# Pinning layer 2's loads, PSUM operands for the half sums and a mask by matmul in a four-layer graph network

## Chip, core and metric

The kernel runs on one core of a Trainium2 chip. The metric is the time of one execution on the device in microseconds (us), the median of several. The core has five engines that run their own instruction streams: TensorE (PE; its weight loads are shown apart as PEld), VectorE (DVE), ScalarE (ACT), GpSimd (POOL) and SyncE (SP), which here issues all DMA transfers.

## What is computed

Four graph layers follow each other over x, 32 batches of 512 nodes with 128 features. Each normalises, applies a relu and adds its result to x. All use one 512x512 matrix adj. Cut to what matters here:

```python
# layer 0: attention over the pattern of adj
m = adj > 0
idx = cumsum(m.reshape(-1)) - 1
A = where(m, e[0][idx], NEG)            # NEG = -9e15; e has 256 entries, an index past the end takes the last
A = softmax(A, axis=1)
out = (A * eye) @ h0 + (A * (1 - eye)) @ h1 + bias      # h0 = h W[0], h1 = h W[1]
# layer 1: x0, x0 adj and its Chebyshev step, each times a block of Theta, relu
# layer 2: weights = adj * adj; messages = weights^T relu(h psi); two dense layers
# layer 3: scores from h q k^T h^T, tanh, exp, times adj, divided by the row sum, times h v
```

## The kernel before

Two batches make a tile q (0 to 15). The 512x512 matrices are multiplied by a scheme of seven products per pair instead of eight, which needs sums and differences of the four 256x256 quarters of the left matrix ("half sums", `sum_steps`) and of the right one (`rt_...`). The preparation builds layer 0's attention matrix, its transpose `attT` and the half sums of that; then rounds `r` of layer 0 follow, two tiles each.

The loads that layers 2 and 3 need:

```python
def load_crossed(dst, src):
    for b in range(NQR):                       # NQR = 4
        nc.sync.dma_start(dst[:, b, :], src.rearrange("(a b c) w -> b a c w", a=NT, c=QR)[b])   # L99
# [cut]
def square():
    sq = square_tile("sq")                     # one of four 512x512 buffers
    load_crossed(sq, adj)
    adjTx.append(square_tile("adjTx"))
    load_crossed(adjTx[0], adjT_d)
    yield
    for i in range(NT):                        # sq becomes adj * adj, on GpSimd
        # [cut]
    yield from sum_steps(sq, "sq")
# [cut] the order in which the program is written from the last round of layer 0 on:
waiting = [[next_layer, layer0_last(), layer1(1)]]        # next_layer is layer1(0)
waiting += [[layer1(q)] for q in range(2, NQ)]
waiting[5].append(square())
# each iteration adds one entry and steps every active generator once
```

Engines PE, DVE, ACT and POOL run the preparation and all rounds of layer 0 but the last in the order of the source (a manual schedule). What follows is ordered by the scheduler of the framework, which works with modelled times; transfers are ordered by it throughout, except those that are pinned, as the later loads of x are.

In layer 0 the features of a tile reach their transposed form hT by VectorE's 32x32 transpose (`hb`), a transfer to DRAM (`d_hT`, L269) and one back (`hT`, L272); the first three tiles are transposed on TensorE. `p_g` (L385) is the product of hT and W[1].

Layer 0's mask and scores, in the preparation (`m` is 1 where adj > 0):

```python
att = square_tile("att")
for t in range(NT):                            # (m - 1) * -NEG: 0 where m is 1, 9e15 where it is 0 (least is sought)
    nc.gpsimd.tensor_scalar(att[:, t, :], m[:, t, :], -1.0, -NEG, OP.add, OP.mult)      # L455
# [cut]
nc.gpsimd.tensor_scalar(elastn, elast, -1.0, None, OP.mult)        # minus the last entry of e
us = [prep.tile([P, N], F32, tag="u", name=f"u_{t}", bufs=NT) for t in range(NT)]
def entries(t):
    nc.scalar.mul(us[t], m[:, t, :], elastn)                       # L521
    nc.gpsimd.tensor_add(att[:, t, :], us[t], att[:, t, :])        # L522
entries(0); entries(1)                         # [cut] entries(2), entries(3) after go(normal[0])
# [cut] normal[q]: the normalised h of tile q, eight ACT instructions (L230)
go(normal[1])
bias(0)                                        # a GpSimd addition to x (L395)
for kk in range(NK):                           # NK = 2
    nc.vector.tensor_scalar(at_row[:, kk, :], ...)                 # L565
    nc.vector.tensor_scalar(at_col[:, kk, :], ..., OP.is_equal, OP.mult)                # L566, 0 or -1
for kk in range(NK):
    for i in range(3):
        nc.vector.tensor_scalar(at_part[:, i, kk, :], ...)         # L569

def score_rows(t):
    ph = bank(f"p_first_{t}")                  # a PSUM bank
    for kk in range(NK):                       # L581: -1 at each of the first 256 entries
        nc.tensor.matmul(ph, at_row[:, kk, blk(t)], at_col[:, kk, :], start=(kk == 0), stop=(kk == NK - 1))
    pv = bank(f"p_val_{t}")                    # L585: six matmuls, the values of e in three bf16 parts
    # [cut]
def softmax_rows(t):
    ph, pv = scores[t]
    u = us[t]
    nc.vector.scalar_tensor_tensor(u, ph, elastn, att[:, t, :], OP.mult, OP.add)        # L592
    nc.vector.tensor_tensor_reduce(u, pv, u, ..., OP.add, OP.min, least[:, t : t + 1])  # L593
    nc.scalar.activation(u, u, AF.Exp, ...)                        # L594
```

The end of the preparation:

```python
pt = [bank(f"p_attT_{j}") for j in range(NT)]  # the transposed attention matrix, in four PSUM banks
# [cut] transposes, p_g of two tiles, rt_g of round 0 (GpSimd, L311), p_adiag
for j in range(NT):
    (nc.vector.tensor_copy if j % 2 else nc.scalar.copy)(attT[:, j, :], pt[j])          # L637
nc.scalar.copy(adiag, p)                       # L638
go(normal[2])                                  # eight ACT instructions
go(sum_steps(attT, "att", nc.vector))

def sum_steps(mat, name, eng=nc.gpsimd):
    a11, a12 = mat[:, 0:2, 0:H], mat[:, 2:4, 0:H]                  # H = 256
    a21, a22 = mat[:, 0:2, H:N], mat[:, 2:4, H:N]
    # [cut] s1, s2, s4: tiles in SBUF
    for out, op, p, q in ((s1, OP.add, a21, a22), (s2, OP.subtract, s1, a11),
                          (a21, OP.subtract, a11, a21), (s4, OP.subtract, a12, s2)):
        tc.keep_in_program_order(eng.tensor_tensor(out, p, q, op))                      # L290
        yield
```

Round 0 then takes products in the order a11 (`p_l_a`), s2 (`p_l_c`), s1 (`p_l_d`), the changed a21, a12, a22, s4 (L337). Ahead of the second TensorE transposes h[2] (`p_hT`, L248). `hd` (GpSimd, L656) feeds the diagonal's products (L709). `cheb` is layer 1's second matrix, also made along the way.

Of the kernel before, what the change touches and what calls it, by code (L numbers as in the profile page):

```python
# [9 lines left out]
F32 = mybir.dt.float32  # L10
F16 = mybir.dt.float16
BF16 = mybir.dt.bfloat16
AF = mybir.ActivationFunctionType
OP = mybir.AluOpType
AX = mybir.AxisListType

P = 128
QR = 32
# [6 lines left out]
def kernel(  # L25
# [37 lines left out]
    nc = tc.nc  # L63
    B, N, D = x.shape
    NT = N // P
    NE = e_l0.shape[1]
    NK = NE // P
    NQ = B // 2

    const = ctx.enter_context(tc.tile_pool(name="const", bufs=1))  # L70
# [6 lines left out]
    def bank(name):  # L77
        return psum.tile([P, 512], F32, tag="bank", name=name)
# [4 lines left out]
    def blk(t):  # L83
        return slice(t * P, (t + 1) * P)


    def square_tile(name):
        return const.tile([P, NT, N], F32, tag="square", name=name, bufs=4)
# [7 lines left out]

    def load_crossed(dst, src):
        for b in range(NQR):
            nc.sync.dma_start(dst[:, b, :], src.rearrange("(a b c) w -> b a c w", a=NT, c=QR)[b])  # L99

    adj_s = square_tile("adj_s")
    adj_r = adj.rearrange("(t p) j -> p t j", p=P)
# [37 lines left out]
    elast = const.tile([P, 1], F32, name="elast")  # L140
# [22 lines left out]
    prep = prep_scope.enter_context(tc.tile_pool(name="prep", bufs=1))  # L163
# [9 lines left out]
                   allow_small_or_imprecise_dtypes=True)  # L173
    ident = const.tile([P, P], F32, name="ident")
    make_identity(nc, ident)
    eps = const.tile([P, 1], F32, name="eps")
    nc.vector.memset(eps, EPS)
    nc.scalar.activation(prep.tile([P, 1], F32, name="powers"), eps, AF.Exp)
# [99 lines left out]
    H = N // 2  # L278
    sums = {}

    def sum_steps(mat, name, eng=nc.gpsimd):

        a11, a12 = mat[:, 0:2, 0:H], mat[:, 2:4, 0:H]
        a21, a22 = mat[:, 0:2, H:N], mat[:, 2:4, H:N]
        extra = const.tile([P, 3, 2, H], F32, tag="sums", name=f"sums_{name}", bufs=3)
        s1, s2, s4 = extra[:, 0], extra[:, 1], extra[:, 2]
        sums[name] = {1: a11, 2: a12, 3: s4, 4: a22, 5: s1, 6: s2, 7: a21}
        for out, op, p, q in ((s1, OP.add, a21, a22), (s2, OP.subtract, s1, a11),
                              (a21, OP.subtract, a11, a21), (s4, OP.subtract, a12, s2)):
            tc.keep_in_program_order(eng.tensor_tensor(out, p, q, op))  # L290
            yield

    def right_blocks(half, name, engs):

        right = {}
        for _ in right_steps(half, name, engs, right):
            pass
        return right
# [117 lines left out]
    def go(steps, n=99):  # L416
        for _ in range(n):
            if next(steps, steps) is steps:
                return
# [24 lines left out]
    m = prep.tile([P, NT, N], BF16, name="m")  # L444
# [4 lines left out]
    rch = prep.tile([P, NT], F16, name="rch")  # L449
    nc.vector.tensor_copy(rch, rc)  # L450


    att = square_tile("att")
    for t in range(NT):
        nc.gpsimd.tensor_scalar(att[:, t, :], m[:, t, :], -1.0, -NEG, OP.add, OP.mult)  # L455
    pt = [bank(f"p_adjT_{j}") for j in range(NT)]
# [8 lines left out]
    for t in range(NT):  # L465
        for s in range(t + 1):
            nc.tensor.matmul(pi[:, t : t + 1], upto[:, s, blk(t)], rch[:, s : s + 1],
                             start=(s == 0), stop=(s == t))
    pc = bank("p_count")
    for t in range(NT):  # L470
        nc.tensor.matmul(pc, rch[:, t : t + 1].to_broadcast([P, P]), upto[:, t, :],
                         start=(t == 0), stop=(t == NT - 1))
# [19 lines left out]
    for kk in range(NK):  # L492
        for t in range(NT):
            nc.tensor.matmul(pb[:, kk : kk + 1], of_row[:, t, blk(kk)], befh[:, t : t + 1],
                             start=(t == 0), stop=(t == NT - 1))
# [3 lines left out]
    at_row = prep.tile([P, NK, N], BF16, name="at_row")  # L499
    at_col = prep.tile([P, NK, N], BF16, name="at_col")  # L500
# [12 lines left out]
            nc.gpsimd.tensor_sub(ecoln, ecoln, part)  # L513
        parts.append(part)
    elastn = prep.tile([P, 1], F32, name="elastn")
    nc.gpsimd.tensor_scalar(elastn, elast, -1.0, None, OP.mult)

    us = [prep.tile([P, N], F32, tag="u", name=f"u_{t}", bufs=NT) for t in range(NT)]

    def entries(t):  # L520
        nc.scalar.mul(us[t], m[:, t, :], elastn)  # L521
        nc.gpsimd.tensor_add(att[:, t, :], us[t], att[:, t, :])  # L522

    entries(0)
    entries(1)
    for kk in range(NK):
        s = prep.tile([P, N], F16, tag="scr", name=f"scr_r{kk}", bufs=2)
        nc.vector.tensor_scalar(s, pc, rows[:, kk : kk + 1], None, OP.is_le, OP.add,
# [6 lines left out]
    for kk in range(NK):  # L535
        w = prep.tile([P, N], F32, tag="scan", name=f"scan_{kk}", bufs=1)
# [9 lines left out]
    project = [project_steps(q, hT[q], copies[q]) for q in range(3)]  # L546
    next(pieces[0], None)
    go(normal[0])
    entries(2)
    entries(3)  # L550
    next(pieces[1])
    next(pieces[1])
    next(pieces[1], None)
# [3 lines left out]
    p = bank("p_qk_t")  # L557
# [20 lines left out]
    def score_rows(t):  # L578
        ph = bank(f"p_first_{t}")
        for kk in range(NK):  # L580
            nc.tensor.matmul(ph, at_row[:, kk, blk(t)], at_col[:, kk, :], start=(kk == 0), stop=(kk == NK - 1))  # L581
        pv = bank(f"p_val_{t}")
        for kk in range(NK):
            for i in range(3):
                nc.tensor.matmul(pv, at_row[:, kk, blk(t)], at_part[:, i, kk, :], start=(kk == 0 and i == 0),  # L585
                                 stop=(kk == NK - 1 and i == 2))
        scores[t] = ph, pv

    def softmax_rows(t):
        ph, pv = scores[t]  # L590
        u = us[t]
        nc.vector.scalar_tensor_tensor(u, ph, elastn, att[:, t, :], OP.mult, OP.add)  # L592
        nc.vector.tensor_tensor_reduce(u, pv, u, 1.0, 3.0e38, OP.add, OP.min, least[:, t : t + 1])  # L593
        nc.scalar.activation(u, u, AF.Exp, bias=least[:, t : t + 1], scale=-1.0,  # L594
                             accum_out=total[:, t : t + 1])

    def scaled_rows(t, u):
        nc.vector.reciprocal(total[:, t : t + 1], total[:, t : t + 1])
        nc.scalar.mul(split(att[:, t, :]), crossed(u), total[:, t : t + 1])
        own = split(att[:, t, :])[:, :, t, :]  # L600
        d = diag[:, t, :].rearrange("p (b c) -> p b c", c=QR)
        nc.gpsimd.tensor_mul(d, own, ident.rearrange("p (b c) -> p b c", c=QR))
        nc.gpsimd.tensor_sub(own, own, d)

    for t in range(NT):
        score_rows(t)
# [3 lines left out]
    nc.tensor.matmul(p_qk[:, :D], qkT[:, 0, :], qkT[:, 1, :], start=True, stop=True)  # L610
    qk = const.tile([P, D], F32, name="qk")
    attT = square_tile("attT")
    for t in range(NT):
        softmax_rows(t)
        if t > 0:
            scaled_rows(t - 1, us[t - 1])
    next(turned[1], None)
# [3 lines left out]
    pt = [bank(f"p_attT_{j}") for j in range(NT)]  # L621
# [11 lines left out]
    p = bank("p_adiag")  # L633
    for t in range(NT):
        nc.tensor.matmul(p[:, blk(t)], ones, diag[:, t, :], start=True, stop=True)
    for j in range(NT):
        (nc.vector.tensor_copy if j % 2 else nc.scalar.copy)(attT[:, j, :], pt[j])  # L637
    nc.scalar.copy(adiag, p)  # L638
    go(normal[2])
    go(sum_steps(attT, "att", nc.vector))  # L640

    prep_scope.close()
    late = ctx.enter_context(tc.tile_pool(name="late", bufs=4))
# [21 lines left out]
    def late_sums():  # L665

        for name, mat in (("adj", adj_s), ("cheb", cheb)):
            yield from sum_steps(mat, name)
# [289 lines left out]
    def square():  # L958

        sq = square_tile("sq")  # L960
# [4 lines that stand above are left out]
        for i in range(NT):  # L965
            s = late.tile([P, N], F32, tag="hs", name=f"sq_{i}", bufs=4)
            nc.gpsimd.tensor_mul(split(s), crossed(sq[:, i, :]), crossed(sq[:, i, :]))
            nc.gpsimd.tensor_copy(sq[:, i, :], s)
        yield from sum_steps(sq, "sq")
# [54 lines left out]
```

## Time and profile before

| | |
|---|---|
| time, median of 3 (lowest, highest) | 986.16 us (985.79, 986.97) |
| span of the profiled execution | 984.6 us |
| mean granted TensorE clock | 0.997 |
| half sums of attT, VectorE, four instructions | 1.80, 1.64, 1.75, 1.75 us |
| m times elastn, ACT, four instructions in two pairs | 1.33 and 1.32 us a pair |
| u and att added, GpSimd, four instructions in two pairs | 2.50 and 2.54 us a pair |
| issues of sq, from | three at 161.83, one at 194.61 us |
| issues of adjTx, from | two at 204.78, two at 206.41 us |

The profile names a group by line, engine and operation, then what is written and read, its shape and how often. "Busy" is the time an engine executes; the time before it, in brackets or in a column, is idle time, with the instruction or transfer that ended it after an arrow. Starts are counted from the start of the span. A tenth row of 40 digits shows the busy share in 40 equal slices of the span.

### The profile page before, as it was taken

What the parts mean: (1) busy time and instruction counts of PE and PEld (TensorE: products, weight loads), DVE (VectorE), ACT (ScalarE), POOL (GpSimd) and SP (SyncE); (2) the same over time, 40 slices, a digit from 0 to 9 for tenths busy, and PEclk for the clock granted to TensorE, in tenths of its full rate; (3) what the DMA queues carried; (4) which work ended last, traced back from release to release, by engine and by line L of the source; (5) the groups of instructions that cost most, each with busy time, mean ns of one, the idle gap of its engine ahead of it and who ended that gap; (6) DMA issues with size and microseconds to landing.
All of it is one profiled execution on the core that took longest, in us unless ns stands there. A gap on an engine that the chain in (4) does not pass through costs nothing.

```text
span 984.6 us, 15193 instructions
## 1 busy us (share of the span) xinstructions
PE 965.6 (98%) x5473; PEld 788.0 (80%) x5474; DVE 597.3 (61%) x1363; ACT 469.6 (48%) x1059; POOL 402.7 (41%) x451
## 2 busy tenths in 40 slices
PE   7999997999999999999999999999999999999998
PEld 3789997889999999999977787777767776777776
DVE  8868887556556565566766666565555444444444
ACT  4675456103232232336766655554574554445553
POOL 6748798562226322221253344444133322233322
PEclk9999999899999999999999999999999999999999
DMA  9155554422213122135333343223132121121111
GB/s 257 49 144 156 150 150 134 128 82 65 66 43 86 43 65 65 47 86 147 86 110 103 115 123 108 74 77 87 44 93 77 46 75 55 54 76 43 54 33 43
DMA packets 83050, 87.10 MB, mean 88 GB/s; under 512 B 6816, under 2 KB 73120, under 8 KB 82976
## 3 DMA queue, kind: packets, MB, share of 16 engines
q1 hardware_dynamic: 82976, 86.14, 31.1%
q8 instruction: 43, 0.70, 0.3%
q14 instruction: 31, 0.25, 0.1%
HBM read 44.70 MB, written 41.42 MB: 87 GB/s over the span
## 4 chain that ended last, share of the span: by engine, by line
PE 93%; DVE 3%; DMA 2%; ACT 1%; issue 0%; SPq 0%; POOL 0%; DVEq 0%; ACTq 0%
PE p_av L944 12%; PE p_l L385 11%; PE p_score L929 11%; PE p_msgT_c L330 4%; PE p_x2T_c L330 4%; PE p_x1T_c L330 4%; PE p_l_c L337 4%; PE p_feat L385 3%; PE p_msgT_d L330 3%; PE p_x1T_a L330 3%; PE p_msgT_a L330 3%; PE p_hv L385 3%; PE p_x2T_d L330 3%; PE p_x1T_d L330 3%; PE p_x2T_a L330 3%; PE p_phi L899 3%
## 5 line engine op out<-in xcount | busy, mean ns | idle before, releaser
L230 ACT ACTIVATE h<-x,sh,rs 128x128 f32<-128x128 f32 x512 | 208.6, 483 | 91.5 <-PE p_x2T_d L330 46.9
L934 POOL TENSOR_TENSOR ex<-ex,adjTx 128x512 f32<-128x512 f32 x64 | 83.2, 1301 | 206.4 <-ACT ex L932 206.4
L930 ACT ACTIVATE ex<-p_score 128x512 f32<-128x512 f32 x128 | 71.8, 587 | 124.6 <-issue 113.0
L944 PEld LDWEIGHTS p_av<-qkh_hv,ex 128*128 128x128 f32 x1024 | 118.5, 191 | 9.4 <-issue 7.4
L944 PE MATMUL p_av<-qkh_hv,ex 128*128 128x129 f32 x1024 | 120.1, 275 | 0.8 <-POOL ex L934 0.8
L929 PE MATMUL p_score<-qkh_hv,hT 128*128 128x512 f32 x256 | 115.2, 593 | 0.0
L264 DVE STREAM_TRANSPOSE hb_hT<-h 128x512 f32<-128x512 f32 x122 | 83.1, 696 | 20.7 <-ACT h L230 20.4
L934 DVE TENSOR_TENSOR ex<-ex,adjTx 128x512 f32<-128x512 f32 x64 | 45.4, 709 | 81.7 <-ACT ex L932 81.7
L202 DVE BATCH_NORM_STATS2 bn<-x 128x6 f32<-128x256 f32 x256 | 93.0, 418 | 1.6
L929 PEld LDWEIGHTS p_score<-qkh_hv,hT 128*128 128x128 f32 x256 | 46.2, 190 | 46.5 <-issue 45.0
L385 PE MATMUL p_l<-th,x12T 128*128 128x128 f32 x512 | 78.1, 275 | 0.0
L932 ACT ACTIVATE ex<-ex 128x512 f32<-128x512 f32 x128 | 76.6, 630 | 1.8
L311 POOL TENSOR_TENSOR rt_h<-h 128x256 f32<-128x256 f32 x32 | 23.2, 726 | 114.1 <-PE p_x2T_d L330 66.6
L385 PEld LDWEIGHTS p_l<-th,x12T 128*128 128x128 f32 x512 | 67.5, 192 | 0.0
L311 POOL TENSOR_TENSOR rt_feat<-feat,feat 128x256 f32<-128x256 f32 x16 | 11.6, 724 | 126.2 <-ACT feat L882 126.2
L654 POOL COPY hs<-hT 128x512 f32<-128x512 f32 x32 | 19.5, 612 | 74.8 <-PE p_l L385 33.0
L385 PE MATMUL p_l<-th,hs 128*128 128x128 f32 x256 | 49.5, 275 | 0.0
L385 PEld LDWEIGHTS p_hv<-vw,hT 128*128 128x128 f32 x256 | 33.6, 192 | 15.3 <-issue 8.1
L894 POOL TENSOR_TENSOR x<-x,phi2b 128x256 f32<-128x256 f32 x64 | 44.9, 732 | 0.0
L358 ACT COPY x12T<-p_x1T_a 128x256 f32<-128x256 f32 x16 | 6.0, 372 | 74.4 <-PE p_x1T_a L330 74.4
L656 POOL TENSOR_TENSOR hd<-hT,adiag 128x512 f32<-128x512 f32 x32 | 41.0, 1312 | 0.0
L385 PEld LDWEIGHTS p_l<-th,hs 128*128 128x128 f32 x256 | 40.0, 192 | 0.8
(224 smaller groups left out, 1992.6 us busy)
## 6 DMA issues: line engine op xcount, KB each, us to landing
d_hT<-hb_hT SPq DMA_DIRECT2D x244, 128.0 KB, 2.4
hT<-d_hT SPq DMA_DIRECT2D x61, 512.0 KB, 3.4
x<-in_x_dram SPq DMA_DIRECT2D x32, 256.0 KB, 5.2
out_dram<-x SPq DMA_DIRECT2D x31, 256.0 KB, 2.3
adj_s<-in_adj_dram SPq DMA_DIRECT2D x4, 256.0 KB
adjT_d<-adjT SPq DMA_DIRECT2D x1, 1024.0 KB
sq<-in_adj_dram SPq DMA_DIRECT2D x4, 256.0 KB
adjTx<-adjT_d SPq DMA_DIRECT2D x4, 256.0 KB
```

The costliest lines, as they stand in the source:

```text
L202: nc.vector.bn_stats(st[:, k].rearrange("p e s -> p (e s)"), xt[q][:, b, t : t + 2, :].rearrange("p t f -> p f t"))
L230: nc.scalar.activation(h[:, b, t, :], xt[q][:, b, t, :], AF.Relu, bias=shift[q][:, i : i + 1], scale=scale[q][:, i : i + 1])
L264: nc.vector.transpose(hb[:, :, b].rearrange("p j t r -> p t j r"), h[:, b].rearrange("p t (j c) -> p t j c", c=QR))
L330: nc.tensor.matmul(p[:, :H], b[:, k, :], a[:, k, :], start=(first and k == 0), stop=(k == 1), skip_group_check=True)
L385: nc.tensor.matmul(p[:, blk(t)], hT(t), w, start=(i == 0), stop=(i == len(terms) - 1))
L656: nc.gpsimd.tensor_mul(split(s), src, split(scale))
L894: tc.keep_in_program_order(nc.gpsimd.tensor_add(xi, xi, spread(phi2b, 2)))
L929: nc.tensor.matmul(ps, hT[:, t, b, :], qkh, start=True, stop=True)
L930: nc.scalar.activation(ex[:, t, :], ps, AF.Tanh, scale=1.0 / (8.0 * math.sqrt(D)))
L932: nc.scalar.activation(ex[:, t, :], ex[:, t, :], AF.Exp, scale=8.0)
L934: eng.tensor_mul(ex[:, t, :], ex[:, t, :], adjTx[0][:, t, :])
L944: nc.tensor.matmul(po[:, i, : D + 1], ex[:, t, blk(i0 + i)], hv[:, t, :], start=(t == 0), stop=(t == NT - 1))
```

## The change

It has three parts. Layer 2's and 3's loads of adj and its transpose get an edge to the instruction traced before them on the same queue, so that the scheduler keeps them behind it. The mask's term `m` times the last entry of e is no longer built by ACT and GpSimd in `att`, but added to the PSUM bank of the first score product as a product of the identity with `m`; VectorE's multiplication by elastn, which was there already, then covers it. And the half sums of attT are taken by a function of their own: it reads one operand of each from the PSUM banks of the transposes, in two halves of 128x256, and one from SBUF; ACT copies three of the four blocks of attT instead of two.

```diff
     def load_crossed(dst, src):
         for b in range(NQR):
-            nc.sync.dma_start(dst[:, b, :], src.rearrange(...)[b])
+            tc.keep_in_program_order(
+                nc.sync.dma_start(dst[:, b, :], src.rearrange(...)[b]))
@@
+    identh = prep.tile([P, P], BF16, name="identh")
+    nc.gpsimd.tensor_copy(identh, ident)
@@
+    def att_sums():
+        # a11 ... s4 and sums["att"] as in sum_steps
+        for out, p, bank_of, half, first in ((s1, a21, 2, 1, False), (s2, s1, 0, 0, False),
+                                             (a21, a21, 0, 0, True), (s4, s2, 2, 0, True)):
+            for k in range(2):
+                b = pt[bank_of + k][:, half * H : half * H + H]
+                if out is s1:
+                    nc.vector.tensor_add(out[:, k], b, p[:, k])
+                elif first:
+                    nc.vector.tensor_sub(out[:, k], b, p[:, k])
+                else:
+                    nc.vector.tensor_sub(out[:, k], p[:, k], b)
@@
-    nc.gpsimd.tensor_scalar(elastn, elast, -1.0, None, OP.mult)
-    # us, entries(t), entries(0), entries(1)
+    nc.vector.tensor_scalar(elastn, elast, -1.0, None, OP.mult)
@@
-    entries(2)
-    entries(3)
@@ score_rows
-            nc.tensor.matmul(ph, ..., stop=(kk == NK - 1))
+            nc.tensor.matmul(ph, ..., stop=False)
+        nc.tensor.matmul(ph, identh, m[:, t, :], start=False, stop=True)
@@ softmax_rows: u is made here and returned
@@
-    for j in range(NT):
-        (nc.vector.tensor_copy if j % 2 else nc.scalar.copy)(attT[:, j, :], pt[j])
+    for j in (0, 1, 2, 3):
+        (nc.vector.tensor_copy if j == 1 else nc.scalar.copy)(attT[:, j, :], pt[j])
@@
-    go(sum_steps(attT, "att", nc.vector))
+    att_sums()
```

## The prediction

> **What bounds the kernel now.** I read the page first, then the waits of TensorE, then the timelines around each wait.
>
> ```profile
> PE 965.6 (98%) x5473; PEld 788.0 (80%) x5474; DVE 597.3 (61%) x1363; ACT 469.6 (48%) x1059; POOL 402.7 (41%) x451
> PE   7999997999999999999999999999999999999998
> ...
> PEclk9999999899999999999999999999999999999999
> ```
>
> TensorE is busy for 965.6 of 984.6 us, so no change that leaves its work alone can bring more than 19.0 us. Of the 40 slices (24.6 us each) only the first, the seventh and the last stand lower, and the eighth has a lower clock. The waits of TensorE, longest first, say where those 19 us lie (the first answer is cut to the first 140 us, the second to 140 to 300 us; columns: total, times, longest).
>
> ```profile
> PE p_adjT L424 <- DMA adj_s<-in_adj_dram: 3.5, 1, 3.5
> PE p_val L585 <- DVE at_part L569: 1.2, 2, 0.9
> PE p_l_c L337 <- DVE sums_att L290: 0.8, 1, 0.8
> PE p_hT L248 <- ACT h L230: 0.7, 1, 0.7
> ...
> PE p_g L385 <- DMA hT<-d_hT: 7.7, 1, 7.7
> ```
>
> One wait is larger than all others that the change could touch: a projection of layer 0 waits 7.7 us for hT. The timelines of TensorE and of the DMA queue around it (start, length, instruction):
>
> ```profile
> 161.83 1.88 SPq L99 DMA_DIRECT2D sq<-in_adj_dram  x3
> 163.95 0.39 SPq L272 DMA_DIRECT2D hT<-d_hT  x1
> ...
> 163.35 1.89 PE L337 MATMUL p_l_a<-g,attT 128*128 128x256 f32 x8
> 165.10 1.99 PE L337 MATMUL p_l_c<-rt_g,sums_att 128*128 128x256 f32 x8
> 174.76 3.76 PE L385 MATMUL p_g<-w,hT 128*128 128x128 f32 x16 [7.67 <-DMA hT<-d_hT]
> 178.31 2.29 PE L337 MATMUL p_l_d<-rt_g,sums_att 128*128 128x256 f32 x8
> ```
>
> Line 99 is layer 2's load of adj. Its values are first multiplied at 296 us, yet it sits in the queue at 162 us, directly ahead of the hT that TensorE needs at 167 us. That hT is issued at 163.95 and released TensorE at 174.7, 10.8 us later; the page's median from issue to landing is 3.4 us. So the scheduler floated the load forward to the moment its buffer came free.
>
> In the preparation (the first 45 us) two places on VectorE matter:
>
> ```profile
> 20.60 0.41 DVE L569 TENSOR_SCALAR at_part<-cols,col_of,part 128x512 bf16<-128x512 f16 x1
> 22.04 1.37 DVE L569 TENSOR_SCALAR at_part<-cols,col_of,part 128x512 bf16<-128x512 f16 x1
> 23.33 1.35 DVE L569 TENSOR_SCALAR at_part<-cols,col_of,part 128x512 bf16<-128x512 f16 x1
> ...
> 21.99 2.54 POOL L522 TENSOR_TENSOR att<-u,att 128x512 f32<-128x512 f32 x2 [0.67 <-ACT u L521]
> ...
> 38.87 1.80 DVE L290 TENSOR_TENSOR sums_att<-attT 128x512 f32<-128x512 f32 x1
> 40.71 1.64 DVE L290 TENSOR_TENSOR sums_att<-sums_att,attT 128x512 f32<-128x512 f32 x1
> ```
>
> The last two at_part instructions take 1.37 and 1.35 us where the first takes 0.41 (their starts are 0.32 to 0.47 apart), and they lie exactly under the two GpSimd additions that build the mask. The half sums take 1.6 to 1.8 us each, while GpSimd runs rt_g and hd without a break.
>
> **What the Trainium skill says.** "SBUF — State Buffer", section "SBUF: two separate sides": VectorE and GpSimd share a pair of ports under an exclusive lock, which a VectorE instruction in a two-port mode or with two SBUF inputs needs; the loser blocks for the whole other instruction. The trace agrees: 1.36 against about 0.4 us above, and, with one operand in PSUM, u_l<-p_l_a,b takes 0.68 us at 45.62 while GpSimd works on hd. "TensorE: Matmul & The Clock Gate", section "What's actually happening": after an idle window of about 3.4 us TensorE's clock falls to half. The trace agrees: after the 7.7 us wait the 16 matmuls of p_g take 3.76 us instead of 1.95, and the granted clock from 175 to 180 us is 0.59. "DMA: Bandwidth & Descriptors", section "Queues, rings and completion order": one engine's transfers share one set of rings, whose descriptors are consumed in order. This fits an hT that queues behind sq.
>
> **The change, part by part.**
>
> *Pinned loads.* The loads get an edge to the instruction traced before them on the queue. square() is first stepped in iteration 5 of the last loop, just after layer 1's hT for q=5 has been traced. In the queue's timeline that hT is the 19th, issued at 264.05 us. So the eight loads go out near 264 us (253 after the gain). What the early load costs now I read from equal points of two rounds: p_l_a's second product follows its first by 8.70 us in a normal round (86.42 to 95.12; 105.66 to 114.35 gives 8.69), and in the disturbed one by 18.82 (163.35 to 182.17). The loss is **10.1 us**: 7.7 wait, 1.8 on p_g, 0.4 on p_l_d, rest small. Without the load the hT would be issued near 161.6 us (its d_hT goes out at 157.57 to 159.32, plus 2.4 to land) and be there by 165, before 167. So all 10.1 us should return. At the new place layer 1's hT of q=5 and q=6 are used only with their p_l blocks, about 40 us after issue (17.4 us per tile, p_l of q=0 at 221), so 2 MB of loads lie beside work. Gain 10.1.
>
> *Mask by a product.* Four ACT multiplications (0.66 each) and four GpSimd additions (1.27) go; VectorE gets one elastn instruction (some 0.1), GpSimd one copy of 128x128 near 2 us, where it idles until 4.2. TensorE gets four more 128x512 bf16 matmuls. Those of p_val follow each other every 0.215 us (six in 1.29). at_part's last two instructions, no longer under L522, end near 22.7 to 23.2 instead of 24.7. bias(0), the next GpSimd instruction of size, needs two h of normal[1]; these move from 24.1 to about 23.1 on ACT, so it starts near 23.9, after at_part. TensorE then does p_first(0) with its third matmul from 21.8 and six p_val until 23.7, and p_first(1) starts at 23.7 instead of 25.17: 1.5 gained. The three later rows pay 3 x 0.215 = 0.65, and elastn 0.1. Left: **0.7 to 0.8 us** at the end of the scores.
>
> *Half sums.* VectorE copies one attT block instead of two (0.6 less) and does eight sums of 128x256 with a PSUM operand. The same form takes 0.42 (x12T<-p_x1T_c,u_x), so 3.4 instead of 6.9 us, and s2 is there after some 1.7 rather than 3.5. But TensorE waited only 0.8 us for s2. Ahead of p_l_c it has transposes of h[2], paced by ACT (h from 38.12 to 41.30, 8 x 0.39), and ACT now copies three attT blocks: 0.52 more, of which 0.15 fills its wait before adiag at 37.64. So h moves up by only about 0.8 - 0.35 = 0.45, the transposes end near 41.1, and p_l_c starts near 41.25 instead of 42.49. Together with the mask the preparation gives about **1.2 us**; the two parts aren't added, since the later one sets the end.
>
> Sum: 10.1 + 1.2 = 11.3 us of 986.16: **974.9 us**, 1.1% less. After 209 us TensorE is busy 771.8 of 776 us, and the change touches nothing there, so an earlier start carries through to the end.
>
> **The rivals.**
> 1. *The wait moves to GpSimd.* From 162 to 176 us and from 190 to 210 us GpSimd has no gap; TensorE's wait let it catch up. Without it, x<-x,u_l (183.86 now, 173.8 then) must wait until 176.04 and the two sums of cheb end near 179.9, where rt_g becomes ready at 180.0 (190.12 - 10.1). It just fits. If not, 1 to 3 us of the gain go: 976 to 978. I give this 15%.
> 2. *The pinned loads hurt at their new place*, by delaying a bounce of layer 1: against it speak the 40 us of slack; 977 to 980. 5%.
> 3. *The sums are the main gain.* VectorE saves 4 us on them, and if the copies were not ACT's, 2 us more might show. Against it: TensorE waits for sums_att only 0.8 us. Then 973.
> 4. *The four matmuls cost 0.86 us and nothing comes back*, because bias(0) or the subtraction in cheb takes at_part's port again: 986.16 - 10.1 + 0.86, less some 0.5 for the sums, 976.4.
>
> **Range and chances.** The loads' term is measured as a lost time and is sure to about 0.5; the preparation may give -0.5 to 2.5; the rivals lengthen the upper side. Eight in ten: 972.5 to 978. Over 2% faster would need 966.4, more than all TensorE waits but the first together, hence 3%; within 2% 96%; slower 1%.
>
> **What would show each step.** Loads: no sq or adjTx near 162 us, all eight together near 253 us, no p_g wait, and a clock of 1.0 throughout. Mask: no instruction of 1.3 us among at_part; p_first(1) near 23.7. Sums: eight VectorE instructions of about 0.42, TensorE waiting before p_l_c for ACT's h rather than for sums_att, p_l_c near 41.2. GpSimd: rt_g of the last round starting right after g. I am wrong if p_g still waits for hT without sq ahead of it, if at_part is still stretched, or if a new wait of over 2 us stands between 160 and 210 us.

## The result and the profile after

The changed kernel takes 974.73 us (974.03 to 975.45) against 986.41 us (985.79 to 986.97), a ratio of 0.9882 with a 95% interval of 0.9865 to 0.9899: 11.7 us or 1.2% less. The prediction was 974.9 us. The total is right; two of its three terms were mis-sized, and the experiments show how far that can be told.

The first lines of the page, then all waits of TensorE that the trace names (total, times, longest):

```profile
PE 963.8 (99%) x5477; PEld 786.5 (81%) x5478; DVE 591.7 (61%) x1367; ACT 467.6 (48%) x1056; POOL 396.4 (41%) x447
PE   8999999999999999999999999999999999999998
...
PE p_adjT L445 <- DMA adj_s<-in_adj_dram: 3.5, 1, 3.5
PE p_av L956 <- POOL ex L946: 0.8, 2, 0.6
PE p_l_c L358 <- DVE u_l L733: 0.4, 1, 0.4
```

The low seventh slice is gone, and the page no longer prints a row for the clock. Of eight waits three are left: at the start, 0.8 us where layer 3's p_av begins (near 694 us), and 0.4 us in the last round of layer 0. (Line numbers shift by up to 21.)

The timelines of TensorE and the DMA queue at the round that used to wait, and at the loads' new place (start, length):

```profile
158.78 0.34 SPq L275 DMA_DIRECT2D hT<-d_hT  x1
...
160.85 1.89 PE L358 MATMUL p_l_a<-g,attT 128*128 128x256 f32 x8
162.60 1.99 PE L358 MATMUL p_l_c<-rt_g,sums_att 128*128 128x256 f32 x8
164.43 1.95 PE L406 MATMUL p_g<-w,hT 128*128 128x128 f32 x16
...
169.67 1.89 PE L358 MATMUL p_l_a<-g,attT 128*128 128x256 f32 x8
...
251.54 0.34 SPq L275 DMA_DIRECT2D hT<-d_hT  x1
251.93 2.56 SPq L100 DMA_DIRECT2D sq<-in_adj_dram  x4
254.85 10.37 SPq L100 DMA_DIRECT2D adjTx<-adjT_d  x4
```

p_g follows p_l_c at once and at full speed (1.95 us instead of 3.76). p_l_a's two products are 8.82 us apart instead of 18.82 (before, the second started at 182.17): 10.0 us. All eight loads now go out behind layer 1's hT of q=5.

In the preparation (VectorE, GpSimd, TensorE, each from its own timeline):

```profile
20.18 2.15 DVE L578 TENSOR_SCALAR at_part<-cols,col_of,part 128x512 bf16<-128x512 f16 x6
35.82 0.92 DVE L308 TENSOR_TENSOR sums_att<-p_attT,attT 128x256 f32<-128x256 f32 x2 [0.30 <-ACT attT L649]
36.66 0.74 DVE L312 TENSOR_TENSOR sums_att<-sums_att,p_attT 128x256 f32<-128x256 f32 x2
...
13.69 0.20 POOL L212 TENSOR_SCALAR sd<-bn 128x8 f32<-128x8 f32 x1 [2.27 <-DVE bn L205]
...
37.47 2.74 PE L251 MATMUL p_hT<-ident,h 128*128 128x128 f32 x8
40.05 1.90 PE L358 MATMUL p_l_c<-rt_g,sums_att 128*128 128x256 f32 x8
```

The six at_part take 2.15 us instead of 4.08, two half sums of 128x256 0.74 (before, one of 128x512 took 1.75). TensorE's transposes of h take 2.74 us, longer than the 2.06 before: they are now what stands ahead of p_l_c.

### The profile page after: what moved, and what is told of

It is laid out like the page before. It is cut to its first block, busy times and chain, and to the rows that moved or that the text cites. A ratio compares the mean times of both kernels' runs of the same rounds, so it can differ in the third digit from the quotient of the medians.

```text
span 972.2 us, 15193 instructions
## 1 busy us (share of the span) xinstructions
PE 963.8 (99%) x5477; PEld 786.5 (81%) x5478; DVE 591.7 (61%) x1367; ACT 467.6 (48%) x1056; POOL 396.4 (41%) x447
## 4 chain that ended last, share of the span: by engine, by line
PE 95%; DVE 2%; ACT 1%; POOL 0%; DMA 0%; issue 0%; DVEq 0%; ACTq 0%
PE p_av L956 12%; PE p_l L406 12%; PE p_score L941 11%; PE p_msgT_c L351 5%; PE p_x1T_c L351 4%; PE p_x2T_c L351 4%; PE p_l_c L358 4%; PE p_feat L406 3%; PE p_msgT_d L351 3%; PE p_x1T_a L351 3%; PE p_msgT_a L351 3%; PE p_hv L406 3%; PE p_x2T_d L351 3%; PE p_x1T_d L351 3%; PE p_x2T_a L351 3%; PE p_g L406 3%
## 5 line engine op out<-in xcount | busy, mean ns | idle before, releaser
L961 DVE SCALAR_TENSOR_TENSOR x<-p_av,rsum,x 128x128 f32<-128x128 f32 x128 | 39.1, 347 | 1.9
```

The costliest lines, as they stand in the source:

```text
L961: nc.vector.scalar_tensor_tensor(xi, po[:, i, :D], rsum[:, i0 + i : i0 + i + 1], xi, OP.mult, OP.add)
```

## How the preparation is compared

The transfers of adj land at different moments from one execution to the next: p_incl, TensorE's first product after adj's transposes, started between 6.95 and 8.52 us in these profiles. I therefore count from p_incl's start to p_l_c's start, after which TensorE runs through. In the kernel before that is 42.49 - 7.46 = 35.03 us, in the changed one 40.05 - 6.95 = 33.10. Between these two profiles the preparation thus gave **1.93 us**; the other 0.5 us by which p_l_c came forward (2.44 in all) is the earlier landing.

This count has a spread of its own. one_floats and two_floats (below) have the preparation of the kernel before, unaltered, and yet need only 34.30 us each. The kernel before, then one_floats (TensorE, GpSimd, VectorE):

```profile
7.46 0.43 PE L467 MATMUL p_incl<-rch,upto 128*128 128x1 f16 x10
36.27 1.27 POOL L311 TENSOR_TENSOR rt_g<-g 128x512 f32<-128x512 f32 x1 [1.51 <-ACT sd L214]
36.44 1.12 DVE L217 SCALAR_TENSOR_TENSOR sh<-bn,rs 128x8 f32<-128x8 f32 x1
42.49 1.97 PE L337 MATMUL p_l_c<-rt_g,sums_att 128*128 128x256 f32 x8 [0.81 <-DVE sums_att L290]
...
8.52 0.45 PE L469 MATMUL p_incl<-rch,upto 128*128 128x1 f16 x10
37.56 0.17 DVE L219 SCALAR_TENSOR_TENSOR sh<-bn,rs 128x8 f32<-128x8 f32 x1
42.82 1.90 PE L339 MATMUL p_l_c<-rt_g,sums_att 128*128 128x256 f32 x8
```

VectorE's `sh`, a small instruction ahead of the half sums, takes 1.08 to 1.12 us where rt_g starts 0.17 to 0.21 us ahead of it (before, pins_only, sums_only, act_queue) and 0.17 in one_floats and two_floats. In these two TensorE waits neither for attT nor for sums_att ahead of p_l_c. In all seven profiles with the new mask sh is short as well. So up to 0.75 us between two rows can be this alone, and how often an execution of the kernel before takes the long form is not known: against 34.30 the changed kernel's gain is 1.2 us, not 1.93. The times of pins_only and of the changed kernel differ by 0.19%, some 1.9 us, but each of the two intervals reaches some 1.6 us to either side, so this fits both.

| kernel | p_incl to p_l_c, us | time, us | ratio to before, 95% interval |
|---|---|---|---|
| before | 35.03 | | |
| pins_only | 35.08 | 977.00 | 0.9901 (0.9886 to 0.9916) |
| one_floats | 34.30 | 979.64 | 0.9925 (0.9911 to 0.9940) |
| two_floats | 34.30 | 984.14 | 0.9972 (0.9960 to 0.9984) |
| mask_only | 32.90 | 984.73 | 0.9978 (0.9969 to 0.9986) |
| sums_only | 34.37 | 986.56 | 0.9995 (0.9987 to 1.0003) |
| mask_and_sums | 33.09 | 985.35 | 0.9986 (0.9979 to 0.9992) |
| changed kernel | 33.10 | 974.73 | 0.9882 (0.9865 to 0.9899) |
| late_powers | 34.24 | 976.01 | 0.9895 (0.9880 to 0.9910) |
| dummy_adds | 37.22 | 977.67 | 0.9903 (0.9886 to 0.9919) |
| act_relieved | 32.86 | 974.25 | 0.9870 (0.9856 to 0.9885) |
| adiag_on_dve | 31.64 | 974.98 | 0.9881 (0.9865 to 0.9898) |

The kernel before took 986.41 to 987.01 us beside these; ratios are the safer comparison across rows, and differences of 0.1% between rows aren't resolved by them.

## Each part alone

**pins_only**: load_crossed as changed, all else as before.

> Before with the pinned loads alone. Theory (the early sq transfers ahead of hT cost 10.1 us, and the later place is hidden): 986.4 - 10.1 = 976.3 us; no wait of p_g for hT, granted clock 1.0, p_l_a's two products of round 6 follow each other by 8.7 to 8.8 us, all eight loads issued together near 254 us. Rival (GpSimd, which used the wait to catch up, becomes the bound): 977 to 979 us, with waits for rt_g between 165 and 200 us.

TensorE's timeline at the same round:

```profile
163.67 1.89 PE L338 MATMUL p_l_a<-g,attT 128*128 128x256 f32 x8
165.49 1.99 PE L338 MATMUL p_l_c<-rt_g,sums_att 128*128 128x256 f32 x8
167.32 1.95 PE L386 MATMUL p_g<-w,hT 128*128 128x128 f32 x16
...
172.56 1.89 PE L338 MATMUL p_l_a<-g,attT 128*128 128x256 f32 x8
```

8.89 us between the two p_l_a, so 9.9 returned; the time fell by 1.0%, which is 9.8 us. No wait for rt_g in the round: GpSimd as the new bound is refuted.

**mask_only**: the mask's part alone, with the old half sums and copies.

> Before with the mask by a product alone; loads and half sums as before. Theory (GpSimd's additions held up both at_part, through the port, and the powers that the first h waits for): 1.5 to 2 us less, some 984.6 us; at_part without instructions of 1.3 us; then TensorE waits longer for sums_att than before, about 1 us, as that part is unchanged. Rival (the four added matmuls eat what at_part gives): within 0.5 us of before.

VectorE's half sums and TensorE in this run:

```profile
36.81 1.55 DVE L292 TENSOR_TENSOR sums_att<-attT 128x512 f32<-128x512 f32 x1
38.40 1.64 DVE L292 TENSOR_TENSOR sums_att<-sums_att,attT 128x512 f32<-128x512 f32 x1
...
38.06 2.54 PE L250 MATMUL p_hT<-ident,h 128*128 128x128 f32 x8
40.44 1.90 PE L357 MATMUL p_l_c<-rt_g,sums_att 128*128 128x256 f32 x8
```

2.1 us in the interval, 0.22% of the time. At the end of the scores, where the prediction had given this part 0.7 to 0.8 us, it is 1.19: TensorE's second group of transposes p_hT starts 21.48 us after p_incl (29.02 - 7.54) instead of 22.67 (30.13 - 7.46). The other 0.9 go with the waits for attT and sums_att (0.2 and 0.8 before) that are gone. One expectation missed: p_l_c does not wait for sums_att at all. s2 is ready at 40.0, as the transposes end. VectorE's `sh` took 0.17 us here instead of 1.12. That the new mask brings this about is not shown, since sh is as short in one_floats and two_floats; against their 34.30 us the mask gives 1.4.

**sums_only**: the half sums and copies as changed, the old mask.

> Before with the half sums from PSUM alone. Theory (TensorE's transposes of h wait for ScalarE, which now has one copy more): only 0.3 to 0.5 us less, some 986.0 us; p_l_c near 42.1 instead of 42.49; eight sums of about 0.4 us. Rival (the sums set the end): 2 us less, 984.4 us, with p_l_c near 40.7.

0.66 us in the interval against the kernel before, with sh long in both (1.08 and 1.12); the time is 0.05% lower, with an interval that includes no change. The rival's 2 us is refuted.

**mask_and_sums**: the changed kernel with load_crossed as before.

> Both changes of the preparation, loads unpinned as before. Theory (the preparation ends 2.0 to 2.4 us earlier and TensorE carries it through to the end): 984.2 us, and the wait of p_g for hT of 7.7 us is still there. Rival (the wait for hT absorbs the gain, since sq's buffer and so its load depend on the same rounds): above 985.5 us.

The interval is 33.09 us, that is 0.2 longer than with the mask alone. So where sh is short, the half sums' part brings nothing in this trace. Of the 1.9 us won here the time shows 1.4 (0.8 to 2.1), 1.2 us short of the 984.2 expected: the wait for hT is 7.9 us, and p_l_a's products lie 19.59 us apart (161.90 to 181.49), 0.8 more than before, since the first matmuls after the wait ran slowly for longer (p_l_d 2.85 us). The rival, that the wait takes the gain altogether, is refuted; that it takes some is seen in this one profile, and the interval of the time leaves it open.

## What the early load costs, block by block

**one_floats** and **two_floats**: one or two of sq's four blocks may still float, the rest is pinned.

```diff
-        load_crossed(sq, adj)
-        load_crossed(adjTx[0], adjT_d)
+        load_crossed(sq, adj, range(n, NQR))                    # pinned
+        load_crossed(adjTx[0], adjT_d)                          # pinned
+        load_crossed(sq, adj, range(n), pinned=False)           # n = 1, 2
```

> Before with all loads pinned but one 256 KB block of sq, which still goes out just ahead of layer 0's hT. Theory (hT stands in line behind sq's blocks; three blocks delay its landing by 10.8 - 3.4 = 7.4 us, 2.5 us a block, and each block's issue by 0.55): hT is there near 168.4 us and p_g waits about 1.3 us; some 977.5 us. Rival A (SyncE's own wait for sq's buffer is what delays hT): hT is issued about as late as before less 1.1 us, lands 3.4 us later, and p_g does not wait. Rival B (a fixed disturbance of any early load): a wait of 7 to 8 us.

> The same with two blocks early. Theory: hT near 171.4 us, p_g waits about 4.3 us; the clock may fall or not[...]; 980.5 to 982 us. Rival A: no wait. Rival B: 7 to 8 us.

The DMA queue and TensorE, first of one_floats, then of two_floats:

```profile
162.10 0.71 SPq L99 DMA_DIRECT2D sq<-in_adj_dram  x1
163.00 0.34 SPq L274 DMA_DIRECT2D hT<-d_hT  x1
169.59 2.02 PE L387 MATMUL p_g<-w,hT 128*128 128x128 f32 x16 [2.23 <-DMA hT<-d_hT]
...
161.86 1.31 SPq L99 DMA_DIRECT2D sq<-in_adj_dram  x2
163.35 0.34 SPq L274 DMA_DIRECT2D hT<-d_hT  x1
172.30 3.75 PE L387 MATMUL p_g<-w,hT 128*128 128x128 f32 x16 [5.16 <-DMA hT<-d_hT]
```

| blocks ahead of hT | hT, issue to TensorE's start, us | wait of p_g | p_g takes | p_l_a to p_l_a |
|---|---|---|---|---|
| 0 (pins_only) | no wait | 0 | 1.95 | 8.89 |
| 1 | 6.6 | 2.2 | 2.02 | 11.28 |
| 2 | 9.0 | 5.2 | 3.75 | 16.73 |
| 3 (before) | 10.8 | 7.7 | 3.76 | 18.82 |

Each block ahead adds to the delay, so neither a fixed disturbance nor SyncE's wait alone explains it. The latter has a share: counted from p_l_a, hT was issued 2.1 us ahead of it in pins_only, 0.6 ahead with one block, and 0.6 after it with three. The waits are 0.9 us above what I had expected, and the times (979.64 and 984.14 us) lie above too, because the clock doesn't scale: after this wait of 2.2 us p_g ran at full speed, after 5.2 at half. The length of the wait alone does not decide it: in act_queue, which follows, another p_g ran at half speed (3.55 us) after a wait of 2.34. From one to two blocks the wait grows by 2.9 us, the loss by 5.4.

**act_queue** asked whether hT stands behind sq in SyncE's line or in the DMA engines that all queues share: the loads are issued by ScalarE.

> Before with all eight loads issued by ScalarE instead of SyncE, still unpinned, so at about the same time. ScalarE then waits for sq's buffer as well, so the time is not the question. Theory A (hT stands behind sq in one queue's line): hT, issued near 161.7 us, lands about 3.5 us later. Theory B (all transfers share the same DMA engines): it lands 6 to 11 us after issue, as in before.

```profile
163.17 0.34 SPq L272 DMA_DIRECT2D hT<-d_hT  x1
163.42 1.16 ACTq L99 DMA_DIRECT2D sq<-in_adj_dram  x1
...
183.09 3.55 PE L385 MATMUL p_g<-w,hT 128*128 128x128 f32 x16 [2.34 <-DMA hT<-d_hT]
```

It missed its aim: ScalarE's stream reached the loads only after hT had gone out, so hT had no block ahead of it. The following bounce hints at the shared engines: six d_hT issued from 168.82 took until 175.97, and its hT could go only at 179.16, 10.3 us after the start; in pins_only the same step took 5.9 us (167.53 to 173.40). Part of that is VectorE's: its second pair of transposes came 4.8 us after the first here, 3.3 in pins_only. The question stays open.

## What the mask held up

**dummy_adds**: the changed kernel with two GpSimd additions that only occupy the port, where entries(2) and (3) stood.

```diff
     next(pieces[1], None)
+    extra = prep.tile([P, N], F32, name="extra")
+    for t in range(2):
+        nc.gpsimd.tensor_add(extra, att[:, t, :], att[:, t, :])
```

> The changed kernel plus two GpSimd additions of 128x512 from att to a tile that nobody reads, at the time of at_part. Theory (at_part loses the port to a GpSimd instruction that reads SBUF): two at_part instructions take 1.3 us again, p_first(1) starts 1 to 1.5 us later than in the changed kernel (22.6 us there), and 975.5 to 976.0 us. Rival (what held up at_part was something else that left with the mask): at_part stays near 0.35 us a piece and the time at 974.7.

GpSimd, VectorE and TensorE:

```profile
21.45 2.20 POOL L565 TENSOR_TENSOR extra<-att 128x512 f32<-128x512 f32 x2
...
22.60 1.20 DVE L581 TENSOR_SCALAR at_part<-cols,col_of,part 128x512 bf16<-128x512 f16 x1
23.72 1.35 DVE L581 TENSOR_SCALAR at_part<-cols,col_of,part 128x512 bf16<-128x512 f16 x1
...
26.91 2.77 PE L598 MATMUL p_val<-at_part,at_row 128*128 128x512 bf16 x6
```

The port is confirmed: at_part is stretched again, and by bias(0) too, which moved under it. It cost more than the expected 0.8 to 1.3 us: 2.9 by the times, 2.1 by the ratios, and 4.1 in the interval of the profiled execution, which was the slowest of the four (978.99 us). There p_first(1) came 18.1 us after p_incl instead of 15.65, and then six p_val took 2.77 us instead of 1.46. The granted clock from 26 to 30 us was 0.57, though no single wait of TensorE here was above 0.9 us. Two of the four executions have a mean clock of 1.000 and took 977.1 and 977.2 us, so the fall is not the whole of the cost.

**late_powers**: the changed kernel with four such additions where entries(0) and (1) stood, ahead of `ln = [...]`.

> The changed kernel plus four GpSimd additions (1.1 us each, to a tile nobody reads) where the mask's first two stood, ahead of the powers that the first h waits for. Theory (the mask's first additions kept GpSimd from the powers: they began 8.05 us after p_incl before the change and 6.74 after it): the powers begin 8.5 to 9.2 us after p_incl, TensorE's transposes of h and the scores shift by as much less 0.3, p_l_c comes 1.2 to 1.8 us later; 976.0 to 976.5 us. Rival (at_part sets the scores alone, as the prediction had it): the transposes move, but p_first(1) and p_l_c stay within 0.4 us.

GpSimd's first power step, before, and in this run:

```profile
15.51 0.20 POOL L209 TENSOR_SCALAR sd<-bn 128x8 f32<-128x8 f32 x1
...
16.28 0.20 POOL L212 TENSOR_SCALAR sd<-bn 128x8 f32<-128x8 f32 x1
```

It begins 8.63 us after p_incl (8.05 before, 6.74 in the changed kernel). p_first(1) starts at 24.44, 16.8 after p_incl and 1.1 later than in the changed kernel, and p_l_c as well; the time is 976.01 us. VectorE's scans and statistics ahead of at_part keep their lengths, so it is the powers that come late. So GpSimd's first two additions, not only the two under at_part, stood on the path, though the four here hold the powers up 0.6 us longer than those two did: VectorE's statistics for the first h are done near 13.9 us in the kernel before, but GpSimd reaches the powers at 15.51.

**quiet_sums**: the kernel before with rt_g of round 0 on VectorE and hd moved behind the first additions to x.

> The kernel before with its SBUF-only half sums, but rt_g of the first round on VectorE and hd later, so that GpSimd does nothing during the half sums. Theory (they take 1.75 us because GpSimd holds the port): four sums of about 0.7 us. Rival (two SBUF operands with these strides are slow by themselves, and PSUM is what helps): about 1.7 us still.

```profile
40.19 0.69 DVE L290 TENSOR_TENSOR sums_att<-attT 128x512 f32<-128x512 f32 x1
40.92 0.69 DVE L290 TENSOR_TENSOR sums_att<-sums_att,attT 128x512 f32<-128x512 f32 x1
41.52 0.68 DVE L290 TENSOR_TENSOR attT<-attT 128x512 f32<-128x512 f32 x1
```

With a silent GpSimd the same SBUF-only sums take 0.69 us instead of 1.75. In the changed kernel two halves with a PSUM operand take 0.74 beside GpSimd's rt_g. So PSUM helps because it avoids the port; as a source it isn't faster.

## What bounds the preparation now

**act_relieved** and **adiag_on_dve** take copies off ScalarE, whose h paces TensorE's transposes.

```diff
-    for j in (0, 1, 2, 3):
-        (nc.vector.tensor_copy if j == 1 else nc.scalar.copy)(attT[:, j, :], pt[j])
-    nc.scalar.copy(adiag, p)
+    nc.scalar.copy(attT[:, 0, :], pt[0])
+    nc.vector.tensor_copy(attT[:, 1, :], pt[1])
+    nc.scalar.copy(adiag, p)                        # adiag_on_dve: on VectorE, after att_sums()
     go(normal[2])
     att_sums()
+    nc.vector.tensor_copy(attT[:, 2, :], pt[2])
+    nc.vector.tensor_copy(attT[:, 3, :], pt[3])
```

> The changed kernel, but ScalarE copies one block of attT instead of three; VectorE copies the last two after the half sums. Theory (h of the third tile on ScalarE paces TensorE's transposes ahead of p_l_c): h starts 1.0 us earlier, p_l_c as well, so 973.7 us, 1.0 less than the changed kernel. Rival (p_l_c then waits for a PSUM bank that the half sums and the late copies hold): p_l_c not earlier, within 0.3 us of the changed kernel.

> As act_relieved, but VectorE also copies adiag, after the half sums, so that ScalarE goes from one copy of attT straight to h. Theory (ScalarE's h paces TensorE; in act_relieved it still waited 0.63 us for adiag): h starts 1.1 us earlier against p_incl than in act_relieved, p_l_c 0.9 to 1.1; 973.3 us. Rival (a PSUM bank or GpSimd's later hd sets the end): no gain over act_relieved's 974.25.

ScalarE in act_relieved, then the queue and TensorE in adiag_on_dve:

```profile
36.36 0.59 ACT L650 COPY adiag<-p_adiag 128x512 f32<-128x512 f32 x1 [0.63 <-PE p_adiag L647]
36.84 3.19 ACT L233 ACTIVATE h<-x,sh,rs 128x128 f32<-128x128 f32 x8
...
48.83 8.79 SPq L272 DMA_DIRECT2D d_hT<-hb_hT  x5
57.81 0.34 SPq L275 DMA_DIRECT2D hT<-d_hT  x1
...
62.23 2.02 PE L406 MATMUL p_g<-w,hT 128*128 128x128 f32 x16 [1.71 <-DMA hT<-d_hT]
```

act_relieved gained only 0.24 us, and h started only 0.23 earlier against p_incl instead of 1.0, because ScalarE then waited 0.63 us for the product that adiag copies. adiag_on_dve removes that wait and brings p_l_c another 1.2 us forward, so ScalarE's h was indeed the pace (sh is short in all three). But the gain is gone 20 us later: p_g waits 1.71 us for hT. The queue's order had changed. The scheduler now put the first d_hT of the next tile ahead of this tile's hT, that d_hT waits for VectorE's transpose at 56.0, and hT, issued at 53.71 in the changed kernel, leaves at 57.81. Again the order of the queue holds up hT, this time by a transfer that is not ready rather than by a long one. Pinning that hT was not tried. The medians of 974.25 and 974.98 us are not told apart from the changed kernel's 974.73; no version was shown to beat it.

## Why the prediction was right, and where it was not

- **Pinned loads, 10.1 us: right.** 10.0 by the two p_l_a, 9.8 by the time of pins_only. The place (near 253 us) and the restored clock came as said. One detail differs: the eight loads did not go out in one piece. The four of adjTx took 10.4 us to issue, where those of sq took 2.6; the next d_hT started at 265.34 and its hT at 277.50. Yet TensorE waited nowhere in layer 1, which fits the 40 us of slack in the prediction.
- **Mask by a product, 0.7 to 0.8 us: the mechanism was right, the term too small.** The port at at_part was as predicted, and the four matmuls too (0.215 us each). The step that failed is "TensorE then does p_first(0) with its third matmul from 21.8": I left the transposes of h where they were. They moved, because the powers on GpSimd no longer stand behind the first two additions; p_first(0) came at 19.91, 13.0 us after p_incl instead of 14.3. At the end of the scores the part gave 1.19 us. bias(0) was also mis-timed: it started at 22.03, not 23.9, 0.3 us before the last at_part ended, and that one had only just begun ahead of it: at_part stayed clear of it by luck.
- **Half sums, 0.45 us on top: not confirmed.** Alone they gave 0.66, after the mask -0.2. The step behind the term, "TensorE waited only 0.8 us for s2", holds only where sh is long: in one_floats and two_floats the old sums cost no wait at all. That TensorE would then wait for ScalarE's h was right, and it is why. The eight sums took 2.8 us (two in 0.74, with starts 0.66 apart), not 3.4.
- **Sum of the preparation, 1.2 us against 1.93** (or 1.2, against the preparation with the short sh). The two errors partly cancel. The gain was 11.7 us where 11.3 was predicted, and the kernel before was measured 0.25 us slower than the 986.16 that the prediction started from; that the total is within 0.2 us is in part luck, beside a spread of 1.4 us in the changed kernel's own times.
- **Rivals.** GpSimd fits, as closely as said: its sums of cheb end at 177.32 and rt_g starts 0.30 us after. The other three didn't come: no wait in layer 1, the sums are not the main gain, and at_part keeps its port (its longest instruction takes 0.54 us, beside GpSimd's subtraction in cheb at 20.03).

## What to carry to other kernels

A load that nobody needs yet is not free: look in the queue's timeline for what stands behind it, and measure its cost from equal points of two rounds, as the wait alone (7.7 us) misses what the clock takes afterwards. An in-order queue whose order a scheduler chooses from modelled times has to be reread after every change, also one that has nothing to do with transfers. A small gain read from one profile each needs a second profile of the same code beside it: here unaltered code ran in two forms 0.75 us apart. And before an instruction of a slow engine is dismissed as hidden, ask what stands behind it on that engine: the mask's first additions delayed the powers, which the prediction had not listed as a cost.

## What the runs showed that I had not expected

- TensorE's clock fell to 0.57 in dummy_adds without a wait above 0.9 us; from 20 to 26 us it had been busy for 3.6 of 6 us. A row of short waits was enough. With act_queue's 2.34 us this says that one long idle window, as the prediction had it, is not the only way to lose the clock.
- The landing of the loads of adj moves p_incl by up to 1.6 us from one execution to the next (6.95 to 8.52 us), as much as the smaller parts of this change are worth.
- Whether rt_g starts 0.2 us ahead of sh or beside it goes with 0.75 us of the preparation.
- Contention takes from both sides: rt_g's last two additions on GpSimd took 1.72 and 1.71 us beside SBUF-only half sums in mask_only, 1.28 each in the changed kernel.
